# Products that nobody reads, put in front of and between the first steps of a state-space recurrence

## The chip, the cores and the metric

The kernel runs on one core of a Trainium2 chip. The core has a matrix engine (TensorE, PE in the profile, with its weight loads shown apart as PEld), a vector engine (DVE), a scalar engine (ACT), a general engine (GpSimd, POOL) and a queue engine that starts transfers (SyncE, SP). Each runs its own instructions in order and they wait for each other through semaphores. The metric is the device time of one execution, in microseconds; lower is better. Three runs of the kernel before gave 3023.68, 3031.63 and 3027.67 us, with the median at 3027.67 us.

## The reference, cut to what matters

Two layers work on x of shape 2 x 2048 x 256, in float32. The first adds causal attention and a mixture of experts to x; the second adds a state-space recurrence (Mamba) and a small ternary product. `xn` is the layer norm of x:

```
x  = x + attention(xn) + moe_block(xn)       # 16 heads; 8 experts, the best 2 of each token
xn = layernorm(x)
xz = xn @ in_proj.T ;  xc, z = split(xz)     # 512 + 512 channels
xs = silu(causal_conv4(xc) + conv_b)
dt, B, C = split(xs @ x_proj.T)              # 16 + 16 + 16
dt = softplus(dt @ dt_proj.T + dt_b)
h[t] = exp(dt[t] * A) * h[t-1] + dt[t] * B[t] * xs[t]     # 512 x 16 states, 2048 steps
y[t] = sum_n h[t] * C[t] + xs[t] * D
out  = x + (y * silu(z)) @ out_proj.T + ternary(xn)
```

The expert block ends with a mix: each token's two expert outputs are weighted and added (`mo`), turned by a 256 x 256 matrix `rot`, and blended by a sigmoid gate with another branch (`ab`) and the residual (`xc`).

## The kernel before, in words

The program has three stretches: attention, the experts (tiles of 256 routed tokens, written to `y_d` in device memory), and the function `mix_and_state_space`, which is the only one the change touches. There the sequence is cut into eight units, four chunks of 512 tokens for each of two batch rows. For a unit, `mix(at)` gathers the two expert rows of each token, mixes, adds and normalises; `ahead(at)` makes projection, convolution and dt; and then come 16 steps of the recurrence. All three are generators, and a hand-written loop at the end of the function steps through them, so that the next units' preparation lies between the steps of the present unit. For unit 0 there is nothing to lie between: `mix(0)` is run through, then ten steps of `ahead(0)` alternate with ten of `mix(1)`, and so on, before the first recurrence step. This is the opening.

What happens in the opening, with the lines that the timeline shows:

- Preamble (up to L1285): weights are loaded, constants made. Among it are the ternary weights: `wt` is loaded behind some twenty small loads on SP (L1262), ACT takes its absolute value (L1264), DVE sums it (L1266), and TensorE sums over partitions, `absum` (L1268); DVE then makes `tern` (L1270 to L1275). `wt` lies in the buffer `k`, which the next tile of that tag, `ab`, needs.
- `mix(0)`: eight gathers of expert rows into `ys` by POOL (L1321), eight scalings by ACT (L1330), their sum by POOL (L1335, `mo`, in place in the half `ys[:, 0]`), loads of `ab` and `xc` (L1337, L1339), eight transposes (L1346, `moT`), the gate (L1354 and L1357, eighteen matmul instructions of one to four columns), the rotation `pn` (L1381), DVE's additions (L1388), POOL's addition (L1398), the layer norm's statistics (L1404, L1405), and its application on ACT (L1418), and eight transposes `tr` (L1426).
- `ahead(0)`: the projection `in` (L1304), the convolution, half of it on DVE and half as products `cv` (L1465), one Silu over all (L1480), the product `xp` (L1485), the first dt product (L1513), softplus of the first 128 channels in short steps between ACT and DVE (L1514 to L1522), and eight products `over` (L1536) that spread dt and dt*x over the partitions, copied out by ACT and DVE in turn.
- Then the first `bb` (L1759), `uh` (L1772) and the scan `hh` (L1862).

A product of float32 operands is two matmul instructions and two weight loads in the trace. Products of the opening write tiles from the pool `ps_m`, tag `mm`, of which there are two buffers; `mm()` hands out the next one, `issued()` keeps the copy that empties a product back until the next product has been issued, and `settle()` issues the copies that are held.

Line order: the part from `tc.manual_schedule()` (L1803) on keeps its written order on each engine. The preamble before it is ordered when the program is built, by what is ready. The trace shows it: ACT's eight scalings (L1330) run before the preamble's L1227 and L1264.

Of the kernel before, what the change touches and what calls it, by code (L numbers as in the profile page):

```python
# [19 lines left out]
P = 128  # L20
# [81 lines left out]
def tile_model(ctx: ExitStack, tc: tile.TileContext, t, out):  # L102
# [55 lines left out]
    with ExitStack() as c0:  # L158
# [176 lines left out]
        experts(tc, t, col, row, ident, ones, xa, xa_d, rot, rw, x_d, y_d, routes)  # L335

    mix_and_state_space(
        tc, t, col, row, ident, ones, rot, routes, sab, rw, y_d, ab_d, xa_d, out_tiles
    )
# [827 lines left out]
def mix_and_state_space(tc, t, col, row, ident, ones, rot, routes, sab, rw, y_d, ab_d, xa_d, out_tiles):  # L1167
# [10 lines left out]
    nc = tc.nc  # L1178
# [7 lines left out]
    with ExitStack() as ctx:  # L1186
# [80 lines left out]
        ps = ps_m.tile([P, 1], F32, tag="mm", name="absum")  # L1267
# [20 lines left out]
        def settle(n=0):  # L1288
            while len(held) > n:
                take, ps = held.pop(0)  # L1290
                take(ps)

        def mm(name, shape=(P, CH)):
            settle(1)
            return ps_m.tile(list(shape), F32, tag="mm", name=name)

        def issued(ps, take):
            settle(0)
            held.append((take, ps))

        def project(m, xnT, name):
            ps = mm(name)
            for k in range(2):
                nc.tensor.matmul(  # L1304
                    ps,
                    lhsT=w_in[:, k, m * P : (m + 1) * P],
                    rhs=xnT[:, k, :],
                    start=(k == 0),
                    stop=(k == 1),
                )  # L1310
            return ps

        def mix(at):
# [4 lines left out]
            ys = one.tile([P, TOP, QT, D], F32, tag="ys", name=f"ys_{u}")  # L1318
# [9 lines left out]
            for e in range(TOP):  # L1328
                for i in range(QT):
                    nc.scalar.activation(  # L1330
                        ys[:, e, i, :], ys[:, e, i, :], AF.Copy, scale=wts[:, e, n0 + i : n0 + i + 1]
                    )
                yield
            mo = ys[:, 0]
            nc.gpsimd.tensor_tensor(mo, mo, ys[:, 1], ALU.add)  # L1335
# [3 lines left out]
            nc.sync.dma_start(xc, xa_d[:, n0 : n0 + QT, :])  # L1339
            yield  # L1340

            moT = ys[:, 1].rearrange("p (k i) d -> p k (i d)", k=2)
            for k in range(2):
                ps = mm(f"moT_{u}_{k}")
# [8 lines left out]
            ps = mm(f"gate_{u}", (P, QT))  # L1353
            nc.tensor.matmul(ps, lhsT=ident, rhs=sab[:, n0 : n0 + QT], start=True, stop=False)  # L1354
            for i in range(QT):
                for k in range(2):
                    nc.tensor.matmul(  # L1357
                        ps[:, i : i + 1],
                        lhsT=moT[:, k, i * P : (i + 1) * P],
                        rhs=rw[:, k : k + 1],  # L1360
                        start=False,
                        stop=(i == QT - 1 and k == 1),
# [13 lines left out]
            for h in range(2):  # L1376
                ps = mm(f"pn_{u}_{h}", (P, 2, D))
# [18 lines left out]
            yield  # L1396
            settle()
            nc.gpsimd.tensor_tensor(xc, xc, ab, ALU.add)  # L1398
            yield

            mv = one.tile([P, QT, 2], F32, tag="mv", bufs=2, name=f"mv3_{u}")
# [21 lines left out]
            for k in range(2):  # L1423
                ps = mm(f"tr_{u}_{k}")
# [9 lines left out]
        def ahead(at):  # L1434
# [7 lines left out]
            for m in range(NB):  # L1442
                issued(
                    project(m, xnT, f"in_{u}_{m}"),
                    lambda ps, m=m: nc.scalar.copy(xr[:, m, DC - 1 :], ps),
                )
                yield
# [3 lines left out]
            for m in range(NB):  # L1451
                if at == 0 and m < NB // 2:
                    x, tap = xs[:, m, :], col("conv_w")[:, m * DC : (m + 1) * DC]
# [9 lines left out]
                ps = mm(f"cv_{u}_{m}")  # L1463
                for k in range(DC):
                    nc.tensor.matmul(  # L1465
                        ps,
                        lhsT=taps[:, m * DC + k, :],
                        rhs=xr[:, m, k : k + CH],
                        start=(k == 0),
                        stop=(k == DC - 1),  # L1470
# [6 lines left out]
                )  # L1477
                yield
            settle()
            nc.scalar.activation(xs, xs, AF.Silu)  # L1480
            yield

            ps = mm(f"xp_{u}", (XR, CH))
            for m in range(NB):
                nc.tensor.matmul(  # L1485
                    ps, lhsT=w_x[:, m, :], rhs=xs[:, m, :], start=(m == 0), stop=(m == NB - 1)
# [9 lines left out]
            def second_part(ps=ps):  # L1496
                nc.vector.tensor_tensor(
                    parts[B1:XR, :], ps[B1:XR, :], parts[B1:XR, :].bitcast(F32), ALU.subtract
                )
                nc.sync.dma_start(c_d, xp[DR : DR + DS, :])  # L1500
# [5 lines left out]
            if at == 0:  # L1506
                second_part()

                spare = one.tile(full, F32, tag="zs", name="spare")
                s0, over = spare[:, 0, :], spare[:, 1, :].rearrange("p (q c) -> p q c", q=4)  # L1510
                v = dt[:, 0, :]
                ps = mm("dt_0")
                nc.tensor.matmul(ps, lhsT=w_dt[:, 0:P], rhs=xp[0:DR, :], start=True, stop=True)  # L1513
                nc.scalar.activation(v, ps, AF.Identity, bias=col("dt_b")[:, 0:1])  # L1514
                nc.scalar.activation(s0, v, AF.Abs)
                nc.scalar.activation(s0, s0, AF.Exp, scale=-1.0)
                nc.vector.scalar_tensor_tensor(v, v, 0.0, s0, ALU.max, ALU.add)
                nc.scalar.activation(s0, s0, AF.Identity, bias=1.0)
                nc.vector.scalar_tensor_tensor(v, s0, 1.0, v, ALU.subtract, ALU.subtract)
                nc.scalar.activation(s0, s0, AF.Ln)  # L1520
                nc.vector.tensor_tensor(v, s0, v, ALU.subtract)
                nc.vector.tensor_tensor(s0, v, xs[:, 0, :], ALU.mult)  # L1522
                yield
                settle()
                for q in range(4):
                    nc.vector.tensor_copy(
                        over[:, q, :].rearrange("p (r c) -> p r c", r=4),
                        ident[:, C4 * q : C4 * (q + 1)].unsqueeze(1).to_broadcast([P, 4, C4]),
                    )

                def spread_by_matmul(m, dt, dx, both):
                    dd = m_["dd", m] = two.tile([P, 2, 4, CH], F32, tag="dd", name=f"dd_0_{m}")
                    for q in range(4):
                        for i, x in enumerate((dt, dx)):
                            ps = mm(f"over_{m}_{q}_{i}")
                            nc.tensor.matmul(ps, lhsT=over[:, q, :], rhs=x, start=True, stop=True)  # L1536
                            issued(
                                ps,
                                lambda ps, q=q, i=i: (
                                    nc.vector.tensor_copy if i and both else nc.scalar.copy  # L1540
                                )(dd[:, i, q, :], ps),
                            )
                        if q == 3:
                            settle()
                        yield

                for _ in spread_by_matmul(0, v, s0, True):
                    pass
                yield
            for m in range(1 if at == 0 else 0, NB):  # L1550
                if at and m == 1:
                    second_part()
                ps = mm(f"dt_{u}_{m}")
                nc.tensor.matmul(  # L1554
                    ps, lhsT=w_dt[:, m * P : (m + 1) * P], rhs=xp[0:DR, :], start=True, stop=True
# [89 lines left out]
        def behind(at):  # L1645

            (c, b), m_ = units[at], of[at]
            if at > 0:
                gated(at - 1, slice(0, NB - 1))
            yield  # L1650
            if at > 0:
                gated(at - 1, slice(NB - 1, NB))
            yield
            out = leave(at - 1) if at > 0 else iter(())
            for _ in range(4):
                next(out, None)
                yield
            for _ in out:
                pass
            zs = m_["zs"] = one.tile(full, F32, tag="zs", name=f"zs_{b}_{c}")  # L1660
            for m in range(NB):
                issued(
                    project(NB + m, m_["xnT"], f"z_{b}_{c}_{m}"),
                    lambda ps, m=m: nc.scalar.copy(zs[:, m, :], ps),
                )
                yield
            settle()
            nc.scalar.activation(zs, zs, AF.Silu)
            yield
# [131 lines left out]
                nc.scalar.copy(of[at]["xs"][:, n // 4, :], of[at]["y"])  # L1801

        ctx.enter_context(tc.manual_schedule())  # L1803
        mixes = [mix(at) for at in range(len(units))]
        aheads = [ahead(at) for at in range(len(units))]
        for _ in mixes[0]:
            pass
# [22 lines left out]
        for G in range(NG):  # L1830
            at, n = divmod(G, NU)
# [154 lines left out]
```

## Time and profile before

| | |
|---|---|
| three runs, median | 3027.67 us (3023.68 to 3031.63) |
| profiled execution: its time, its span | 3027.19 us, 3025.5 us |
| mean granted TensorE clock | 0.908 |
| PE, DVE, ACT, POOL busy | 86%, 68%, 53%, 38% of the span |
| end of the experts' last product | about 1873.2 us |
| first `moT`, last `pn`, first `tr` | 1894.72, ends 1906.84, 1914.72 us |
| first `in`, first `xp`, first `over` | 1917.35, 1936.45, 1952.07 us |
| first scan of the recurrence | 1965.66 us |

How to read it: times are us from the start of the span. The page cuts the span into 40 slices, and the row PEclk gives in tenths the share of its full clock that TensorE was granted. The windows view gives, for a stretch, PE's busy time, its number of instructions in brackets, the granted clock and the transfer engines' share. The timeline lists instructions, merged where they follow each other, with the idle time before them and what ended it. A matmul's busy time includes waiting in its pipe, so a small matmul looks longer than the time its columns take.

### The profile page before, as it was taken

How to read it: one execution, taken by the hardware profiler on the slowest of the kernel's cores; microseconds unless marked ns; L12 is line 12 of the kernel's file. 1: busy time of each engine (PE TensorE's matmuls, PEld its weight loads, DVE VectorE, ACT ScalarE, POOL GpSimd, SP SyncE). 2: the span in 40 equal slices, each digit the busy share in tenths (PEclk: the TensorE clock that was granted, in tenths of full speed). 3: DMA queues.
4: the chain of work that ended last, by engine and by line, in shares of the span. 5: the costliest groups of instructions: out<-in, count | busy, mean ns of one | idle time of the engine just before them, and what ended most of it. 6: DMA issues, size and time to landing. Idle time of an engine off the chain costs nothing. (4 is left out here: it accounts for less than half of the span.)

```text
span 3025.5 us, 39961 instructions
## 1 busy us (share of the span) xinstructions
PE 2616.7 (86%) x15021; PEld 1484.5 (49%) x15021; DVE 2063.7 (68%) x2630; ACT 1592.7 (53%) x2546; POOL 1159.4 (38%) x864
## 2 busy tenths in 40 slices
PE   6879999999999999799999997677878788887846
PEld 4544444445444444587888886332333243333313
DVE  6569888887888886232110101368999999999996
ACT  3425666665666666321322222466766666766542
POOL 4302221110001101111112111268897887978875
PEclk9969999999999999899999998787887878889758
DMA  8842432232222300543445554124443635445340
GB/s 294 209 145 68 85 76 50 41 45 50 36 29 37 49 2 15 183 139 125 149 165 183 193 187 110 59 68 95 116 109 87 153 76 126 105 98 132 81 108 14
DMA packets 120614, 309.58 MB, mean 102 GB/s; under 512 B 28464, under 2 KB 70832, under 8 KB 102880
## 3 DMA queue, kind: packets, MB, share of 16 engines
q1 hardware_dynamic: 100496, 206.57, 29.0%
q0 software_dynamic: 18576, 99.24, 9.7%
q8 instruction: 122, 2.00, 0.3%
q10 hardware_dynamic: 1344, 1.16, 0.1%
q14 instruction: 76, 0.62, 0.1%
HBM read 228.51 MB, written 78.38 MB: 101 GB/s over the span
## 5 line engine op out<-in xcount | busy, mean ns | idle before, releaser
L776 ACT ACTIVATE p<-s 128x1024 f32<-128x1024 f32 (+3 forms) x640 | 564.3, 900 | 337.9 <-PE s L763 256.3
L678 DVE TENSOR_REDUCE best<-m 128x2 f32<-128x1024 f32 (+3 forms) x640 | 670.7, 1063 | 68.4 <-PE m L665 58.6
L1874 POOL TENSOR_TENSOR hh<-hh,cc 128x2048 f32<-128x2048 f32 x128 | 580.0, 4531 | 10.4 <-POOL carry L1873 0.2
L1862 DVE TENSOR_TENSOR_SCAN hh<-decay,uh 128x2048 f32<-128x2048 f32 x128 | 565.9, 4421 | 22.7 <-ACT decay L1748 9.6
L718 PE MATMUL pv<-p,v 128*17 128x256 f32 (+1 forms) x4608 | 377.6, 373 | 4.3 <-ACT raw L749 3.8
L1748 ACT ACTIVATE decay<-dd,a_neg 128x511 f32<-128x511 f32 x512 | 332.9, 712 | 54.6 <-DVE hh L1862 54.0
L1137 ACT ACTIVATE hT<-h,b1s 128x256 f32<-128x256 f32 x296 | 137.6, 473 | 384.4 <-PE h L1130 384.3
L781 POOL TENSOR_SCALAR_AFFINE_SELECT p<-p 128x256 f32<-128x256 f32 x184 | 74.4, 406 | 664.6 <-ACT p L776 663.9
L1151 DVE TENSOR_TENSOR yt<-o,b 128x512 f32<-128x512 f32 x37 | 25.6, 692 | 437.4 <-PE o L1143 437.4
L1772 DVE TENSOR_TENSOR uh<-dd,bb 128x2048 f32<-128x2048 f32 x128 | 293.6, 2294 | 19.7 <-PE bb L1759 10.7
L665 PE MATMUL m<-k,q 64*128 64x512 f32 (+3 forms) x1280 | 281.5, 424 | 27.4 <-ACT p L776 15.2
L763 PE MATMUL s<-q,k 64*128 64x512 f32 (+3 forms) x1280 | 285.9, 433 | 21.7 <-DVE best L678 17.7
L1130 PE MATMUL h<-xT,w 128*128 128x256 f32 x1184 | 276.1, 387 | 19.5 <-ACT hT L1137 7.7
L1143 PE MATMUL o<-w,hT 128*128 128x256 f32 x1184 | 262.1, 379 | 0.0
L1093 POOL DMA_INDIRECT w<-in_w,wrow x74 | 71.2, 962 | 478.1 <-PE h L1130 255.0
L1130 PEld LDWEIGHTS h<-xT,w 128*128 128x128 f32 x1184 | 227.0, 194 | 54.7 <-issue 8.4
L763 PE MATMUL s<-tops,onesr 64*128 64x512 f32 (+3 forms) x1280 | 247.3, 367 | 0.0
L1143 PEld LDWEIGHTS o<-w,hT 128*128 128x128 f32 x1184 | 225.2, 190 | 30.7
L1789 PE MATMUL y<-hh,sel 128*32 128x512 f32 x1024 | 163.7, 716 | 76.8 <-POOL hh L1874 76.6
L763 PEld LDWEIGHTS s<-q,k 64*128 64x128 f32 x1280 | 125.0, 185 | 167.7 <-DVE best L678 58.5
L665 PEld LDWEIGHTS m<-k,q 64*128 64x128 f32 x1280 | 127.3, 188 | 146.5 <-ACT p L776 88.8
L718 PEld LDWEIGHTS pv<-p,v 128*17 128x17 f32 x4608 | 106.8, 96 | 181.5 <-issue 114.0
(344 smaller groups left out, 3492.6 us busy)
## 6 DMA issues: line engine op xcount, KB each, us to landing
dd<-dd_d SPq DMA_DIRECT2D x120, 512.0 KB
q<-qk_d SPq DMA_DIRECT2D x128, 128.0 KB
k<-qk_d SPq DMA_DIRECT2D x128, 128.0 KB
x_d<-zero SPq DMA_DIRECT2D x6, 1664.0 KB
xg<-x_d SPq DMA_DIRECT2D x37, 256.0 KB
y_d<-yt SPq DMA_DIRECT2D x37, 256.0 KB
qk_d<-qp SPq DMA_DIRECT2D x16, 512.0 KB
qk_d<-kp SPq DMA_DIRECT2D x16, 512.0 KB
```

The lines of the kernel that those rows point to most:

```text
L665: nc.tensor.matmul(ps[:, h, 0:n], lhsT=qT[hs, qs], rhs=kT[hs, c * CH : c * CH + n], start=True, stop=True, tile_position=(HP * h, 0),)
L678: nc.vector.tensor_reduce(best[:, i, :, c], ps[:, :, 0:n], AX.X, ALU.max)
L718: nc.tensor.matmul(pv[r0 : r0 + HS + 1, lo - f * HC : HC], lhsT=v[:, b * TPB + kb, 2 * pr + h, :], rhs=pt[:, h, lo:hi], start=(kb == 0), s ...
L763: nc.tensor.matmul(ps[:, h, off:CH], lhsT=(kT[hs, kb * P : (kb + 1) * P], onesr[hs, :])[i], rhs=(qT[hs, j * CH + off : (j + 1) * CH], tp[h ...
L776: nc.scalar.activation(pt[:, :, off:CH], ps[:, :, off:CH], AF.Exp, scale=float(HS) ** -0.5)
L1130: nc.tensor.matmul(ph, lhsT=w1[:, k * DF + f * P : k * DF + (f + 1) * P], rhs=xT[:, k, :], start=(k == 0), stop=(k == 1),)
L1143: nc.tensor.matmul(po[:, h, :], lhsT=hT[:, f, h * P : (h + 1) * P], rhs=w2[:, f * D : (f + 1) * D], start=(f == 0), stop=(f == NF - 1),)
L1748: nc.scalar.activation(decay[G % 2][:, q, 1:], of[at]["dd", n // 4][:, 0, q, 1:], AF.Exp, scale=a_neg[:, q, n : n + 1],)
L1772: nc.vector.tensor_tensor(uh, of[at]["dd", n // 4][:, 1], of[at]["bb", n].to_broadcast(full), ALU.mult)
L1789: nc.tensor.matmul(of[at]["y"][C4 * q : C4 * (q + 1), :], lhsT=sel, rhs=hh[:, q, :], start=False, stop=(g == 3), tile_position=(0, C4 * q),)
L1862: nc.vector.tensor_tensor_scan(hh.rearrange("p q c -> p (q c)"), decay[G % 2].rearrange("p q c -> p (q c)"), uh.rearrange("p q c -> p (q c)"),
L1874: nc.gpsimd.tensor_tensor(hh, hh, m_["cc", g].to_broadcast(full), ALU.mult)
```

## The change

A helper `busy(name, n, x)` is added: it issues the held copies, takes the next `mm` buffer, and issues n products of the identity matrix with x into it (x is four copies of the identity, 512 columns, unless given). No instruction reads these results, so the output of the kernel is unchanged. It is called at seven places, in the first unit alone: eight products before everything of `mix(0)`; two after each of the eight scalings, with the scaled slice of `ys` (256 columns) as x; two before `moT`; seven after POOL's addition of L1398 in the written order; three before the Silu; five after the first dt product. Nothing is removed and nothing else is moved.

```diff
+        def busy(name, n, x=None):
+
+            settle()
+            x = ident.unsqueeze(1).to_broadcast([P, 4, P]) if x is None else x
+            ps = mm(name, x.shape)
+            for _ in range(n):
+                nc.tensor.matmul(ps, lhsT=ident, rhs=x, start=True, stop=True)
+
         def project(m, xnT, name):
...
                         ys[:, e, i, :], ys[:, e, i, :], AF.Copy, scale=wts[:, e, n0 + i : n0 + i + 1]
                     )
+                    if at == 0:
+                        busy(f"busy_{e}_{i}", 2, ys[:, e, i, :])
                 yield
...
             yield
 
+            if at == 0:
+                busy("busy_mo", 2)
             moT = ys[:, 1].rearrange("p (k i) d -> p k (i d)", k=2)
...
             nc.gpsimd.tensor_tensor(xc, xc, ab, ALU.add)
+            if at == 0:
+                busy("busy_ln", 7)
             yield
...
             settle()
+            if at == 0:
+                busy("busy_xs", 3)
             nc.scalar.activation(xs, xs, AF.Silu)
...
                 nc.scalar.activation(v, ps, AF.Identity, bias=col("dt_b")[:, 0:1])
+                busy("busy_dt", 5)
                 nc.scalar.activation(s0, v, AF.Abs)
...
         ctx.enter_context(tc.manual_schedule())
+        busy("busy_0", 8)
         mixes = [mix(at) for at in range(len(units))]
```

## The prediction

> **What bounds the kernel now.** I read the page's slices first, then the chain of waits over the opening, then PE's timeline there, and last windows of 3.41 us, the grid on which the granted clock changes in this trace. Over the whole span PE is 86% busy, but that is an average over other stages; the opening (1873 to 1966 us) is a single chain that hops between engines, and the rest of the span, about 1060 us, begins when it ends. So a microsecond taken off this chain is one off the end. On the chain, word for word:
>
> ```profile
> 1894.31 0.56 PE absum L1268 x2
> 1894.86 1.81 PE moT L1346 x8
> ...
> 1897.13 3.42 PE gate L1357 x16
> 1900.55 6.30 PE pn L1381 x16
> ...
> 1936.45 5.40 PE xp L1485 x8
> ...
> 1952.07 8.97 PE over L1536 x14
> ```
>
> These PE pieces are what a clock can shorten. The windows show at which clock they ran; columns are PE's busy time (instructions), clock, DMA share, GB/s:
>
> ```profile
> core 0: us, PE busy (x), PEclk, DMA share, GB/s
> 1871.81:1875.23 3.42, 1.35 (x7) 1.00 0.13 47
> 1875.23:1878.64 3.41, 0.00 (x0) 0.50 0.84 258
> ...
> 1899.12:1902.53 3.41, 3.41 (x12) 0.50 0.58 232
> 1902.53:1905.95 3.42, 3.42 (x9) 0.50 0.00 0
> 1905.95:1909.36 3.41, 0.89 (x4) 1.00 0.00 0
> 1909.36:1912.77 3.41, 0.00 (x0) 0.50 0.12 36
> ...
> 1933.25:1936.67 3.42, 0.22 (x1) 1.00 0.00 0
> 1936.67:1940.08 3.41, 3.41 (x5) 0.50 0.00 0
> 1940.08:1943.49 3.41, 2.69 (x6) 1.00 0.03 5
> 1943.49:1946.91 3.42, 1.31 (x9) 1.00 0.23 71
> 1946.91:1950.32 3.41, 0.00 (x0) 0.50 0.45 145
> ```
>
> The reader is to see two things. A window with 1.35 us of work or less is followed by one at half clock, and one filled with products by one at full clock (2.61 us at 1929.84 was enough to stay, 1.67 at 1950.32 not to rise). And `moT`, the gate, nearly all of `pn`, most of `xp` and the first three `over` pairs ran at half. Two rows of the timeline give what bounds the start of TensorE's work:
>
> ```profile
> 1888.81 2.10 ACT L1330 ACTIVATE ys<-ys,wts 128x256 f32<-128x256 f32 x5 [1.87 <-DMA ys<-y_d,slots]
> 1894.31 0.56 PE L1268 MATMUL absum<-part,ones 128*128 128x1 f32 x2 [21.15 <-DVE part L1266]
> ```
>
> **Prices.** The change adds 41 products (82 matmuls and as many weight loads), all on PE's queue, and no transfer. A 512-column product is two instructions: `cv` has 16 in 7.03 us at full clock, so 0.86 us; at half, `over` starts at 1952.07, 1953.90 and 1955.61, so about 1.72. A 256-column product is half of each (`pn`: 16 instructions in 6.43 us, nearly all at half clock).
>
> **busy_0**, 8 products, 6.9 us at full clock: from about 1874, where PE is past the branch behind the experts, to 1880.9. It lies in an idle stretch of 21.15 us and costs nothing unless it comes late (third rival).
>
> **busy_0_0 to busy_1_3**, two products each, 0.86 us full, 1.72 half. Each waits for its scaling. The first three sit in gaps of 2 us or more between scalings. Their windows hold 1.3 and then about 2.5 us of work, so the clock is half again from 1885.5. The last five scalings end between 1889.3 and 1890.9, one every 0.42 us, faster than even a full clock eats products, so a backlog forms. Five pairs from 1889.3: 3.0 us at half clock do 1.7 of them; that window is 88% filled, and I take it to raise the clock at 1892.29; the other 3.3 take 2.8 us, to 1895.1. POOL's sum (L1335) now also waits for the four products that read the half it overwrites, the last done at 1891.0; POOL started at 1891.00 anyway, so 0 to 0.3 us, covered by the backlog. `absum`, ready at 1894.1, finds its place inside the backlog: 0.4 us, to 1895.5.
>
> **busy_mo**, two products, 1.7 us, to 1897.2. So `moT` starts 2.5 us later than its 1894.72. Bounds: 1.2 late if the clock rises a window sooner, 4.2 if one later. Waiting behind it on PE are gate and `pn`; behind `absum` wait DVE's `tern` steps and, on SP, the loads of `ab` and `xc` (1896.92 now, landed by about 1901). Some 1.2 us later, they are still in time for ACT's L1395.
>
> **The stretch from moT to the end of pn** takes 1906.84 - 1894.72 = 12.1 us. At full clock: half of `moT` 0.57 (the eight at 1943.98 take 1.13), two ACT copies of 0.58, which makes 1.8; fifteen gate instructions at half of 3.56/16 us, 1.65; `pn` 16 at 0.21, 3.4; in all 6.9. Gain 5.2. Bounds: 5.2, and 2.7 where the gate, which has next to no columns and left PE at half clock for 3 us of "busy" time, drops the clock for `pn`. With windows as recorded, 1897.2 puts products on both sides of the gate into its windows (2.2 us in each), so I take 5.2.
>
> **busy_ln**, seven products, 6.0 us behind `pn`; `tr` comes 7.88 us behind `pn`, set by DVE, POOL and ACT, which the change leaves alone. 1.9 us of cover; with two products at half clock 0.2. What it buys: `tr` is paced by ACT (one per 0.49 us), and with the 1.9 us ahead of it the window still holds about 1 us of work. So half clock again when `in` starts, as now. Before, `in` lost 1.1 us and `tr` 0.5. Bounds: +1.6 if held, -1.4 if `in` meets two half-clock windows; I take 0, the present row.
>
> **busy_xs**, three products, 2.6 us in the 4.00 us between `cv` and `xp`. The remaining pause is 1.4 us, so the window stays filled enough. `xp` takes 3.5 instead of 5.4: gain 1.9, bounds 0 and 1.9.
>
> **busy_dt**, five products, 4.3 us. They wait for the buffer that DVE's L1497 still reads (as the `moT` of unit 1 does now, 1943.98), so 1943.9 to 1948.2, and that `moT` behind them to 1949.3; ACT copies it at 1950.24, in its order, so nothing waits. A pause of 2.8 us remains before `over`; at half clock three pairs cost 5.2 us instead of 2.85 (0.95 each later on). With the chain 4.6 us earlier, one half-clock window covers 2.8 us of `over`: gain 1.0, bounds 0 and 2.3.
>
> **Sum:** -2.5 + 5.2 + 0 + 1.9 + 1.0 = 5.6 us. The profiled execution took 3027.19 us (span 3025.5 and 1.7 around it), 0.5 below the median. 3027.19 - 5.6 = 3021.6; on the median's footing 3022.1 us. A difference under 0.3%, 9.1 us, is not told from no change here, and the three runs lie 8 us apart.
>
> **Where the skill differs.** In the row at 1871.81 PE idled only some 2 us and the clock was half afterwards. The Trainium skill, "TensorE: Matmul & The Clock Gate", section "Why this matters for your kernels", sets the limit at idle gaps of over about 3 us. By that rule every pause left (1.9, 1.4, 2.8 us) would hold the full clock and the sum would be that of the first rival. The same page, Part 1, says that the window runs free and its phase differs from run to run, which speaks against any fixed gain; one trace cannot show this.
>
> **Rivals.** (1) All pauses are held: `moT` 1.2 late, then 5.2 + 1.6 + 1.9 + 2.3: gain 9.8 us, 3017.9. For it: windows of 1.82 us (2015.17) kept the clock; against: 1.31 and 1.35 did not. (2) The gain is lost between: the gate drops the clock (2.5 less) and `in` meets two slow windows (1.4 less): 1.7 left, 3026.0, no change. For it: the gate's rows do not raise a clock; it depends on where windows fall. (3) Slower: `absum` is placed ahead of `busy_0` in PE's queue. PE then stands until 1894.3 and all 15.5 us of products follow, with up to two windows of half clock (1.7 to 3.4 more): `moT` 18 us late, and 18 - 8.1 = 10 slower, 3037.6. It decides from 8.1 us of products behind `absum`, which is `busy_0` among them. For it: `absum` is written first. Against: ACT's scalings overtook the preamble's L1227 that was not ready, so `absum`, which needs that same ACT queue, should also be overtaken. If only the last five pairs stand behind it, `moT` is about 8 late and the end unchanged, which is the second rival's time.
>
> **Chances.** The forecast, 3 to 9 us faster, 0.55; rival 1 0.15; rival 2 (both ways to no change) 0.20; rival 3 0.10. Faster by over 0.3% takes rival 1's upper half and the forecast's tail, 0.16; slower takes rival 3 and a little of rival 2's spread, 0.11; within, 0.73. Range: rival 1 less 3 us of spread, 3015, to rival 2 plus 5, 3031; the forecast's own is 3018 to 3025.
>
> **What would show it.** Right: full clock from about 1892 to 1909; `pn` in about 3.4 us; `moT` near 1897 with `absum` among or behind the scaled products; `xp` in 3.5 us; first scan near 1960. Wrong: half clock in the window behind the gate, `tr` waiting for `busy_ln`, `over` waiting for `busy_dt`, PE idle before `absum` with `busy_0` behind it.

## The result, and the profile after

The change made the kernel slower: 3040.78 us (median of six runs, 3036.85 to 3047.20) against 3028.09 us before, a ratio of 1.0045 with a 95% interval of 1.0033 to 1.0057, or some 12.7 us. The prediction was 3022.1 us with a range of 3015 to 3031. The third rival, priced at 3037.6 us and given one chance in ten, is what happened.

TensorE's timeline of the opening after the change (start, duration, engine, line, operation, tiles, count, idle time before and what ended it):

```profile
1889.69 0.56 PE L1268 MATMUL absum<-part,ones 128*128 128x1 f32 x2 [22.56 <-DVE part L1266]
1890.11 9.46 PE L1307 MATMUL busy<-ident 128*128 128x512 f32 x16
1899.41 7.07 PE L1307 MATMUL busy<-ys,ident 128*128 128x256 f32 x32
1906.32 1.88 PE L1307 MATMUL busy_mo<-ident 128*128 128x512 f32 x4
1908.03 1.04 PE L1358 MATMUL moT<-ident,ys 128*128 128x128 f32 x8
...
1909.60 1.97 PE L1369 MATMUL gate<-rw,ys 128*128 128x1 f32 x16
1911.42 5.39 PE L1393 MATMUL pn<-rot,ys 128*128 128x256 f32 x16
1916.65 6.17 PE L1307 MATMUL busy_ln<-ident 128*128 128x512 f32 x14
...
1946.13 3.69 PE L1501 MATMUL xp<-xs,w_x 128*112 128x512 f32 x8 [1.42 <-ACT xs L1496]
```

The reader is to see the first line: `absum` still stands first in TensorE's queue, and TensorE idles 22.56 us for it with 26 products that need nothing from it lined up behind. They then take 1908.03 - 1890.11 = 17.9 us, on the path. The chain of waits of the changed kernel says the same, where before had 0.6 us between `absum` and `moT`:

```profile
1889.69 0.56 PE absum L1268 x2
1890.25 16.23 PE busy L1307 x48
1906.48 1.72 PE busy_mo L1307 x4
1908.20 0.45 PE moT L1358 x4
```

POOL's sum of the expert rows was held as well, since eight of the products, two behind each of the first four scalings, read the half that it overwrites (the prediction counts four). It ended at 1905.5 us, before the last products did, so it is not what `moT` waited for:

```profile
1903.18 2.36 POOL L1345 TENSOR_TENSOR ys<-ys 128x1024 f32<-128x1024 f32 x1 [22.57 <-PE busy L1307]
```

Counted from the end of the experts' last product (1873.2 us before, 1867.1 after; that stretch itself differs by up to 8 us between the profiled executions of this case):

| us | before | after |
|---|---|---|
| to `moT` | 21.6 | 40.9 |
| from `moT` to the end of `pn` | 12.1 | 8.8 |
| from `moT` to the first scan | 70.9 | 63.3 |
| to the first scan (the opening) | 92.5 | 104.2 |
| from the first scan to the second | 13.3 | 15.2 |

So behind `moT` the products did what they were priced for: 7.7 us gained up to the first scan (8.1 in the forecast). But 19.3 us were lost ahead of it, and 1.8 us more were lost at the second scan. Another 0.8 us went at the third scan: it came 20.5 us behind the second before, 21.3 after, and there DVE waited 3.13 instead of 2.32 us for a small step on ACT; why that step was later was not followed up. These differences come from one profiled execution each; that of the changed kernel was the fastest of its six.

### The profile page after: what moved, and what is told of

The parts are those of the page before. It is cut to its first block, busy times and chain, and to the rows that moved or that the text cites. A ratio compares the mean times of both kernels' runs of the same rounds, so it can differ in the third digit from the quotient of the medians.

```text
span 3035.1 us, 40135 instructions
## 1 busy us (share of the span) xinstructions
PE 2635.5 (87%) x15103; PEld 1493.5 (49%) x15103; DVE 2063.2 (68%) x2630; ACT 1592.8 (52%) x2546; POOL 1159.1 (38%) x864
## 5 line engine op out<-in xcount | busy, mean ns | idle before, releaser
L1789 DVE TENSOR_TENSOR uh<-dd,bb 128x2048 f32<-128x2048 f32 x128 | 293.6, 2294 | 19.3 <-PE bb L1776 10.4
L665 PE MATMUL m<-k,q 64*128 64x512 f32 (+3 forms) x1280 | 280.4, 422 | 27.4 <-ACT p L776 15.2
L1130 PE MATMUL h<-xT,w 128*128 128x256 f32 x1184 | 274.5, 385 | 19.3 <-ACT hT L1137 7.6
```

Source lines behind the costliest of these rows:

```text
L665: nc.tensor.matmul(ps[:, h, 0:n], lhsT=qT[hs, qs], rhs=kT[hs, c * CH : c * CH + n], start=True, stop=True, tile_position=(HP * h, 0),)
L1130: nc.tensor.matmul(ph, lhsT=w1[:, k * DF + f * P : k * DF + (f + 1) * P], rhs=xT[:, k, :], start=(k == 0), stop=(k == 1),)
L1789: nc.vector.tensor_tensor(uh, of[at]["dd", n // 4][:, 1], of[at]["bb", n].to_broadcast(full), ALU.mult)
```

## The experiments

Theory 1: the loss is the place of the front products in the queue, behind `absum`. Theory 2: it is the products themselves, wherever they stand. Times are medians, beside runs of the kernel before on the same chip (3029.05, 3027.93 and 3027.98 us in the three groups); "opening" is from the end of the experts' last product to the first scan, in the one profiled execution.

### absum behind the products

```diff
-        nc.vector.tensor_reduce(part, tern, AX.XY, ALU.add)
-        ps = ps_m.tile([P, 1], F32, tag="mm", name="absum")
-        nc.tensor.matmul(ps, lhsT=ones, rhs=part, start=True, stop=True)
...
+        def ternary():
+            nc.vector.tensor_reduce(part, tern, AX.XY, ALU.add)
+            ps = mm("absum", (P, 1))
+            nc.tensor.matmul(ps, lhsT=ones, rhs=part, start=True, stop=True)
...
+            if at == 0:
+                ternary()
             mo = ys[:, 0]
```

> The changed kernel with the sum over partitions of the ternary weights (absum, and DVE's tern steps behind it) written behind the sixteen scaled products, ahead of busy_mo; all 41 products stay. Theory 1, the place in the queue: in the changed kernel all front products stand behind absum, which is ready only some 16 us after the experts' end, and this alone makes it slow. Then busy_0 runs right behind the experts, moT comes 1 to 4 us later after the experts' end than in the kernel before (it came 19 us later in the changed one), the 7.7 us that the changed kernel's opening gained from moT to the first scan stay, and the time is 3 to 7 us under the kernel before, about 3023. Theory 2, the products themselves: they hold POOL's sum of the expert rows and TensorE whatever stands ahead of them. Then moT is still 10 us or more late and the time is at or above the kernel before, 3030 to 3040.

The timeline of TensorE:

```profile
1874.40 7.10 PE L1309 MATMUL busy<-ident 128*128 128x512 f32 x16 [0.93 <-DVEq L1162]
...
1889.82 4.58 PE L1309 MATMUL busy<-ys,ident 128*128 128x256 f32 x20 [0.49 <-ACT ys L1340]
1894.65 0.35 PE L1271 MATMUL absum<-part,ones 128*128 128x1 f32 x2 [0.25 <-PE busy L1309]
1894.86 1.96 PE L1309 MATMUL busy_mo<-ident 128*128 128x512 f32 x4
1896.66 1.04 PE L1362 MATMUL moT<-ident,ys 128*128 128x128 f32 x8
...
1900.06 3.70 PE L1397 MATMUL pn<-rot,ys 128*128 128x256 f32 x16
1903.59 6.17 PE L1309 MATMUL busy_ln<-ident 128*128 128x512 f32 x14
```

`busy_0` now runs right behind the experts, and `moT` starts 23.2 us after their end, 1.6 later than before instead of 19.3: theory 1 holds for the loss, with the same 41 products. The time is 3027.08 us, ratio 0.9994 (0.9983 to 1.0005): the 13 us are gone, but no gain can be told, where 3 to 7 us were expected. The opening in this execution was 85.0 us against 92.5, and of those 7.5 us only about 2 show in the time. Where they went is taken up below.

### The later products alone

The calls of `busy_0`, `busy_{e}_{i}` and `busy_mo` are left out; seven, three and five products stay.

```diff
-                    if at == 0:
-                        busy(f"busy_{e}_{i}", 2, ys[:, e, i, :])
...
-            if at == 0:
-                busy("busy_mo", 2)
...
-        busy("busy_0", 8)
```

> The changed kernel without the front products (busy_0, the sixteen scaled ones, busy_mo); seven, three and five products behind pn, cv and the first dt product stay. Both theories: moT as in the kernel before, gate and pn at half clock as there; xp 1.7 to 1.9 us and over 1 to 1.4 us shorter, in about even: 3 us under the kernel before, about 3025, within what can be told. If the later products cost something that the trace of the changed kernel hides (its recurrence took 4 us longer than before), it is at or above 3028.

3028.52 us, ratio 0.9997 (0.9987 to 1.0006): no difference, 3.5 us over the 3025 expected. The opening was 90.8 us; `xp` took 3.7 us as expected, but `in` met more of the half clock (9.4 us, before 8.2), and the second scan came 15.1 us behind the first instead of 13.3.

### Without busy_0

```diff
-        busy("busy_0", 8)
```

> The changed kernel without busy_0; the scaled products and busy_mo still stand behind absum. Theory 1: some 8.6 us of products at full clock, 11 at mixed clocks, are left behind absum, so moT is about 11 us late, of which 7.7 are won back: 3 us over the kernel before, about 3031. Theory 2, in the form that the readers of ys make the loss: nothing changes against the changed kernel, about 3040.

3034.45 us, ratio 1.0023 (1.0012 to 1.0034), halfway between before and after. `moT` came 32.6 us after the experts' end, 11.0 late, as priced, and the opening was 3.2 us longer than before's, as expected. The time is 3.4 us over the expected 3031; the second and the third scan came 1.8 and 0.8 us later behind the one ahead of them than in before, which is most of it. Theory 2 in the form that the readers of `ys` make the loss is out.

### The front products alone

```diff
-            if at == 0:
-                busy("busy_ln", 7)
...
-            if at == 0:
-                busy("busy_xs", 3)
...
-                busy("busy_dt", 5)
```

> The changed kernel without the seven, three and five later products; the front products stay behind absum. Theory 1: moT 18 to 19 us late, gate and pn win back about 3 of it, nothing else does: 15 to 16 us over the kernel before, about 3043. If the later products are what costs, it is faster than the changed kernel, under 3037.

3045.96 us, ratio 1.0052 (1.0036 to 1.0067), 3 us over the expected 3043. Without the later products the kernel is slower still, so these were not the harm.

### Why absum stood first: one line

```diff
-        ps = ps_m.tile([P, 1], F32, tag="mm", name="absum")
+        ps = ps_y.tile([P, 1], F32, tag="y", name="absum")
```

> The changed kernel with one line different: absum writes a buffer of its own (that of y, free until the first step) instead of one of the two of the tag mm. Theory 1 with the cause in the shared buffers: the two buffers of mm are handed out in the written order, absum's is the first, and that alone put it ahead of busy_0. Then busy_0 runs right behind the experts here and moT comes 1 to 4 us later than in before; absum now falls among the pn products, so ab is loaded some 8 us later than it could be and POOL's L1398 waits for it: about 4 us of the gain goes back, time 3022 to 3032. If the order has another cause, busy_0 still waits behind absum, 3040.

```profile
1869.26 7.11 PE L1307 MATMUL busy<-ident 128*128 128x512 f32 x16 [0.93 <-DVEq L1162]
...
1892.17 1.04 PE L1358 MATMUL moT<-ident,ys 128*128 128x128 f32 x8
...
1898.52 0.28 PE L1268 MATMUL absum<-part,ones 128*128 128x1 f32 x2
1898.66 1.11 PE L1393 MATMUL pn<-rot,ys 128*128 128x256 f32 x4
1906.72 8.55 PE L1307 MATMUL busy_ln<-ident 128*128 128x512 f32 x14 [6.95 <-DVE xc L1400]
```

With another buffer for `absum`, and no other line changed, `busy_0` runs 0.93 us after the branch behind the experts, and `absum` falls among the `pn` products, behind 12 of their 16 matmul instructions. So the cause is the shared pair of buffers: `absum` was the first to take one, and `busy_0`, which takes them too, did not come ahead of it. There are two of them, so `busy_0` could have had the second while `absum` held the first; why the order was kept even so is not shown. The time is 3033.62 us, ratio 1.0020 (1.0007 to 1.0032), a little over the expected range. The other reason that was expected shows in the profile: `ab` is loaded behind `absum`, ACT waited 7.30 us for `ab`, and `busy_ln` itself waited 6.95 us for DVE to empty a `pn` buffer. The opening was 93.4 us, 1 to 2 us over before's. But the profiled execution was the fastest of the seven (3025.98 us), so it does not show all of the 6 us by which the median is over before's.

### Two second profiles: where the 7.5 us went

The kernel before, and the one with `absum` behind the products, unchanged.

> The kernel before, unchanged, for a second profile. In the first one the first scan of the recurrence came 92.5 us after the experts' end and the rest took 1059.8 us; the five kernels with added products took 1061.6 to 1066 for that rest. Theory 1a: the rest varies from execution to execution and 1059.8 was a short one: here about 1064, the opening again 92 to 93, the time as before. Theory 1b: the added products make the later steps 4 to 5 us slower: here again about 1060.

> The changed kernel with absum behind the scaled products, once more, for a second profile and more times: its profile showed the opening 7.5 us shorter than before's, its median only 2 us. Theory 1a: the phase of the clock's windows differs between executions, so the opening here is anything from 85 to 90 us, and the time again 2 to 6 us under before. Theory 1b: opening 85 again, and the rest 1065 again, where before has 1060.

Before: 3028.92 us, ratio 1.0001 (0.9989 to 1.0012), opening 91.3 us, rest 1061.1. With `absum` behind: 3025.67 us, 0.9999 (0.9990 to 1.0008), opening 91.9 instead of 85.0, rest 1065.8 instead of 1065.3. The second execution's timeline of the same program:

```profile
1885.26 7.56 PE L1309 MATMUL busy<-ys,ident 128*128 128x256 f32 x20 [1.09 <-ACT ys L1340]
...
1898.09 5.39 PE L1397 MATMUL pn<-rot,ys 128*128 128x256 f32 x16
```

The five scaled pairs took 7.6 us instead of 4.6 and `pn` 5.4 instead of 3.7: the clock's windows fell otherwise. That is theory 1a for the opening, with a wider spread than its 85 to 90. For the rest, the numbers are nearer to theory 1b: both profiles of before have the second scan 13.3 and 13.4 us behind the first, all seven of the kernels with products so far 14.2 (`absum` in its own buffer) to 15.2. That it is the added products that do it does not follow, as is said below. DVE's timeline shows the wait, first of the changed kernel, then of before; the lines below are in DVE's order, with the second scan last:

```profile
1975.84 2.30 DVE L1789 TENSOR_TENSOR uh<-dd,bb 128x2048 f32<-128x2048 f32 x1
1984.51 1.76 DVE L1592 SCALAR_TENSOR_TENSOR dt<-dt,s 128x1536 f32<-128x1536 f32 x1 [6.38 <-ACT s L1589]
...
1986.46 4.42 DVE L1880 TENSOR_TENSOR_SCAN hh<-decay,uh 128x2048 f32<-128x2048 f32 x1
```

```profile
1970.18 2.30 DVE L1772 TENSOR_TENSOR uh<-dd,bb 128x2048 f32<-128x2048 f32 x1
1977.05 1.76 DVE L1575 SCALAR_TENSOR_TENSOR dt<-dt,s 128x1536 f32<-128x1536 f32 x1 [4.57 <-ACT s L1572]
...
1979.00 4.42 DVE L1862 TENSOR_TENSOR_SCAN hh<-decay,uh 128x2048 f32<-128x2048 f32 x1
```

The second scan stands in DVE's queue behind a step of the remaining dt channels, and that step waits through ACT for six matmuls `dt`. These ran in part at full clock before and wholly at half in the changed kernel (TensorE's timeline, before and changed):

```profile
1965.27 0.50 PE L1759 MATMUL bb<-b,selb 48*128 48x512 f32 x1 [2.76 <-DVE uh L1772]
1965.69 3.97 PE L1554 MATMUL dt<-xp_sb,w_dt 16*128 16x512 f32 x6
```

```profile
1970.92 0.79 PE L1776 MATMUL bb<-b,selb 48*128 48x512 f32 x1 [2.76 <-DVE uh L1789]
1971.64 5.48 PE L1571 MATMUL dt<-xp_sb,w_dt 16*128 16x512 f32 x6
```

Which clock they met hangs on the window ahead, with the last `over` products and the first `bb`. In the two profiles of before that window held 1.94 us (1960.56 to 1963.97) and 2.10 us of TensorE's work, and the next was at full clock. In the changed kernel it held 1.62 us and the next was at half. With the front products alone it held 1.86 us (1974.97 to 1978.38), and the next was at half too, with a second scan 15.1 us behind the first, although from `tr` on that kernel issues the same instructions as before. All twelve profiles of this case but the two with the bridge, described below, agree: full clock behind 1.94 us and more, half behind 1.86 and less. So the loss needs no added product near it: it comes when the border of a window cuts this stretch a little later. Whether added products make it likelier, two profiles of before cannot tell.

### Fewer products in front, absum behind moT

```diff
-                        busy(f"busy_{e}_{i}", 2, ys[:, e, i, :])
+                        busy(f"busy_{e}_{i}", 2 - e, ys[:, e, i, :])
...
+            if at == 0:
+                nc.scalar.activation(tern, wt, AF.Abs)
+                nc.vector.tensor_reduce(part, tern, AX.XY, ALU.add)
             mo = ys[:, 0]
...
-            if at == 0:
-                busy("busy_mo", 2)
...
             settle()
+            if at == 0:
+                ternary()
+                ab = one.tile([P, QT, D], F32, tag="k", name=f"ab_{u}")
+                nc.sync.dma_start(ab, ab_d[:, n0 : n0 + QT, :])
```

> Fewer products in front and absum behind moT: busy_0 8, two behind each of the first four scalings, one behind each of the last four, no busy_mo; the absolute value and DVE's sum written behind the scalings, absum, tern and the load of ab behind moT. Theory 1: moT starts as soon as POOL's sum is done, some 3 us sooner than with absum behind the products and 1 us sooner than before, gate and pn at full clock if the gate does not drop it: 3 us under that kernel, 5 to 8 under before, 3021 to 3024. Rival: without busy_mo the window around the gate is too empty, pn runs at half clock and the 3 us go back: 3027.

> The trimmed kernel once more (busy_0 8, two and one behind the scalings, no busy_mo, absum behind moT), for a second profile and more times. If its 3 to 5 us under before are real: 3022 to 3025 again, ratio under 1. The opening between 85 and 90 us from the experts' end to the first scan; the second scan 15 us behind the first, as in all kernels with added products so far, where before has 13.3 and 13.4.

3022.89 us, ratio 0.9991 (0.9981 to 1.0000), and 3024.80 us, 0.9992 (0.9983 to 1.0001); openings 85.2 and 85.0 us, `moT` 20.8 and 22.1 us after the experts' end. About 2.5 us faster by the ratios, at the edge of what can be told, less than expected. In both executions part of `pn` ran at half clock (5.12 and 5.17 us), in the first the gate too (3.55 us): the rival's mechanism.

### Products where the clock falls ahead of dt

```diff
         spread_b(0)
         product(0)
+        busy("busy_bb", 3)
```

> The trimmed kernel with three products more, between the first bb and the second, where TensorE waits 2.75 us for uh. Theory 1c: the gain given back behind the opening (second scan 15.1 instead of 13.3 us behind the first, third 36.5 instead of 33.8) is the six dt matmuls at half clock (5.5 instead of 4.0 us), on which ACT, the DVE step L1575 and, behind it in DVE's queue, the second scan wait. Then dt takes 2.6 to 4 us here, the second scan comes 12 to 13.4 us behind the first, and the time is 2 us under the trimmed kernel. Rival: the gap of before and after has another cause (the loads of dd or cc): 15.1 stays.

> The trimmed kernel with nine products instead of seven behind pn: 7.7 us of the 7.9 us up to tr. If the 1.9 us pause ahead of tr is what lets the clock fall for in, it holds now: in 7 us instead of 7 to 9, the time 0 to 2 us under the trimmed kernel. If products at half clock run into tr, tr comes later: 1 to 2 us over it.

> Both of the last two edits. If they add up: 2 to 4 us under the trimmed kernel, 3018 to 3021, 7 to 10 us under before.

TensorE's timeline of the trimmed kernel with the bridge:

```profile
1957.27 2.84 PE L1307 MATMUL busy_bb<-ident 128*128 128x512 f32 x6
1960.10 0.50 PE L1782 MATMUL bb<-b,selb 48*128 48x512 f32 x1
1960.53 3.71 PE L1577 MATMUL dt<-xp_sb,w_dt 16*128 16x512 f32 x6
```

The bridge gives 3020.60 us, ratio 0.9977 (0.9967 to 0.9987): the second scan comes 13.1 us behind the first, as theory 1c has it, and not 15.1, as the rival has it. The time is some 4.5 us under the trimmed kernel's by the ratios, where 2 was expected, and the intervals just overlap. Over the fourteen profiles that distance goes with the time of the six `dt` matmuls: 11.4 us where they took 3.02, 13.1 to 13.6 where 3.7 to 4.2, 14.2 where 4.80, and 15.1 in all eight where 5.48. Nine products instead of seven behind `pn` give 3022.95 us, 0.9988 (0.9979 to 0.9997), which does not tell it from the trimmed kernel; in its one profile the second scan came after 13.6 us without a bridge, so a favourable phase can do the same. Both edits give 3019.84 us, 0.9975 (0.9966 to 0.9984), second scan 11.4 us behind the first. That is the fastest version here, not told from the bridge alone, 8.1 us under before (3027.98) by the medians and 7.6 by the ratio, and some 21 under the changed kernel.

## Why the prediction was wrong

**The step that failed** is the one on `busy_0`: "It lies in an idle stretch of 21.15 us and costs nothing unless it comes late", with "`absum`, ready at 1894.1, finds its place inside the backlog". It did come late: TensorE idled 22.56 us for `absum`, 17.9 us of products followed, and the term of the sum that stood at -2.5 us for the start of `moT` measured -19.3. I argued from ACT, whose scalings had overtaken the preamble's L1227, that TensorE's queue would be ordered by readiness too. The row was right for ACT. For TensorE there was one more condition, which the code of `mm()` shows and which I had used for `busy_dt` but not here: `absum` and `busy_0` share the two buffers of one tag. The one-line run shows that without this sharing `absum` does not come first.

**Rival 3** had the mechanism, the place and nearly the price: `moT` 18 us late, measured 19.3; gain behind it 8.1, measured 7.7; 10 us slower, measured 12.7. What it lacks is 1.3 us at the front and the second and third scan, 1.8 and 0.8 us, which I had not looked at; with these it comes to some 14, a little over the measured. Its point of decision, 8.1 us of products behind `absum`, held in its sign: with `busy_0` taken out, 11 us of products stood there and some 7 us of loss remained, where that price alone gives 3.

**Had the order been as assumed**, the terms can be read from the kernel with `absum` behind the products. `moT` 2.5 us late, bounds 1.2 to 4.2: measured 1.6 and 4.1. From `moT` to the end of `pn` 6.9 us: 7.1 and 8.8, the second with the drop behind the gate that stood in the bounds (5.4 instead of 3.4 for `pn`). `in`, taken as unchanged at 8.2 with bounds of 1.6 less and 1.4 more: measured 8.1 and 9.4. `xp` 3.5: 3.7. `busy_ln` and `busy_dt` delayed nothing, as priced. `over` gained 2.3 and 0.8 where 1.0 was taken. In the two profiles these terms add up to gains of some 7.5 and 0.5 us on the first profile of before, which is what the openings differ by (85.0 and 91.9 against 92.5). The sum of 5.6 was too high all the same: the two openings average 3.5 us under those of before (92.5 and 91.3), 1.8 us go back at the second scan and 0.8 at the third, and the ratios say 0.3 and 1.8 us. I had let the chain end with the first scan; the clock's price goes on behind it.

**The clock's rule** was weighed right in the changed kernel. There a pause of 1.88 us, followed by thinly spaced transposes, left 1.32 us of work in its window and dropped the clock for `in`, which took 7.9 us against 8.2 before, inside the bounds (windows view: busy time with instructions, granted clock, transfer share, GB/s):

```profile
core 0: us, PE busy (x), PEclk, DMA share, GB/s
1918.75:1922.16 3.41, 3.41 (x9) 1.00 0.00 0
1922.16:1925.58 3.42, 1.32 (x4) 1.00 0.38 115
1925.58:1928.99 3.41, 3.29 (x8) 0.50 0.13 38
```

In the trimmed kernel the same pause (1907.55 to 1909.43) lies inside one window as well, but 1.41 us of filler products stand ahead of it there, and the clock stayed:

```profile
1906.14:1909.56 3.42, 1.54 (x5) 1.00 0.32 89
1909.56:1912.97 3.41, 2.69 (x11) 1.00 0.22 65
```

The Trainium skill's limit of some 3 us of idling ("TensorE: Matmul & The Clock Gate", section "Why this matters for your kernels") is too generous here: in before the clock was half from 1875.23 on, 2.1 us after the experts' last product, and in the changed kernel 1.88 us with thinly spaced transposes behind them were enough. Nor does the pause alone decide, since the same 1.88 us did not drop it in the trimmed kernel. The page's other statement, that the windows run free and differ from run to run (Part 1 of the same page), agrees with the two profiles of one program whose openings differ by 6.9 us.

## What to carry to other kernels

Before work is put into an engine's idle time, look at the instruction at which that engine is idling: what is added must come ahead of it in the queue, and a shared buffer can forbid that as well as a data dependence. Filler products pay only up to the first wait behind them, so follow the chain past the stage that they were meant for. And an effect that hangs on a free-running clock window needs several profiles of the same program: one trace of the opening was 7 us off another.

## What the runs showed of the hardware that was not expected

Matmuls of 16 rows hold the clock badly. In before, four of the six `dt` matmuls (16 rows) and a `bb` (48 rows) kept TensorE busy for 2.12 of 3.42 us in one window (1963.97 to 1967.39), and the clock fell behind it, while 1.82 us of 128-row work (2015.17) kept it. Behind the bridge one window (1959.31 to 1962.72) was filled from end to end, 2.19 us of it by `dt`, and the clock fell behind it all the same. So `dt` began at full clock and took 3.71 us in one execution and 3.02 in another, where six at full clock would take 2.6 (an estimate, at `cv`'s 0.43 us an instruction). That the rows are the reason is read from these windows; no run changed the rows alone.
